# A GIN and a three-layer GAT on one core: blocks of 125 nodes, a hand-kept order, and PSUM operands for VectorE

## The chip, the cores and the metric

The kernel runs on one core of one Trainium2 chip. The metric is the device time of one execution in microseconds (us), taken as the median over several runs. A core has five engines that work side by side, each through its own list of instructions in order: PE (TensorE, matrix products; its weight loads are listed apart as PEld), DVE (VectorE), ACT (ScalarE), POOL (GpSimd) and SP (SyncE, which here only issues transfers). An instruction that waits holds up everything behind it on its engine. Transfers run on 16 DMA engines; SP and ACT issue plain ones, POOL issues those whose rows are named by a table of indices (indirect ones).

## The reference

A graph has N = 3125 nodes with 64 features and E = 103125 directed edges, sorted by destination: 50,000 random pairs in both directions and a loop at each node. Cut to what matters:

```python
h = relu(layernorm(x))
for layer in 1, 2, 3:                      # GIN, MLP widths 64, 128, 64
    agg = segment_sum(h[src] * edge_weight[:, None], dst)
    h = relu((agg + h) @ w1 + b1) @ w2 + b2      # relu between layers
x = x + h
h = relu(layernorm(x))
t = h @ init_w + init_b + mlp(pos_embed(node_vec))   # 128 features
src, dst = with_self_loops(src, dst)
for layer in 0, 1, 2:                      # GAT, 8 heads, widths 256, 256, 128
    xw = (t @ W).reshape(N, 8, C)
    logits = leaky_relu((xw * a_src).sum(-1)[src] + (xw * a_dst).sum(-1)[dst], 0.2)
    e = exp(logits - segment_max(logits, dst)[dst])
    alpha = e / segment_sum(e, dst)[dst]
    g = segment_sum(alpha[:, :, None] * xw[src], dst) + bias
    t = silu(batch_norm(g + t @ adj_w + adj_b))
return x + t @ out_w + out_b
```

## The kernel before

The node axis is cut into NT = 25 blocks of P = 128 (NP = 3200 places, the last block partly empty). The program goes through five stages.

`search` and `slots` sort the edges into slots. Nodes are ordered by their number of edges and packed into 25 groups of 128; group t has `CAPS[t]` slots per node (64 down to 23, 857 columns in all). `weigh(t)` in `slots` compares all pairs of slots of a node (128 × n × n elements on DVE) to add up the weights of repeated sources; `put(t)` then writes one column of 128 weights at a time into a dense adjacency matrix in DRAM, `adj`: 857 indirect transfers from POOL (`scatter`, L943). For GAT the slots are split again. A first edge per (node, source block) is found by a masked maximum over `key`, which gives `tops` and later `lane`: for node d and source block s the row within the block, or a mark in `void` that there is none. The edges that are left, up to 48 a node, are "the others": nodes are ordered by how many they have and packed into 25 groups of 128 with `MORE[t]` columns (44, 24, 22, ... 7; 400 in all), with row numbers in `idx` and destinations in `perm`.

`embed` (L171 to L188) makes the position embedding. `hots` turns `lane` into one-hot matrices: per destination block one DVE comparison against `iota` (L929), 25 PE transposes (L937), ACT copies (L938) and a store to DRAM by SP (L939). Both stand between `slots` and GIN in the code; within one pool the tile framework orders the instructions of each engine by a plan of its own.

`gin` keeps the sums of eight or nine destination blocks in PSUM and streams the dense adjacency past them: per layer 75 loads `adj_t` on SP's queue (L973) and matmuls with the features as weights (L977).

`gat` works in three steps per layer. First the projection: for every block `xw` and the attention terms (a row of W = D + 8 numbers), stored as a table `tab` and `ald_d` in DRAM and kept in SBUF as three bf16 parts, `split`, whose sum is the fp32 value; the dense residual goes to DRAM.

Then `add_edges`, block by block. `gather` picks the first edges' rows with one-hot matmuls: 26 slots (25 source blocks and the node's own loop) of three bf16 parts each (L1078), two slots to a PSUM tile `g`, copied to SBUF by ACT (L1079). The slots come in three parts of 12, 12 and 2 (`parts`); three large buffers `tiles` go round. `weigh` makes the weights: adds on DVE (L1088 to L1092), the leaky ReLU (L206), and in `exps` a maximum, a subtraction (L1181), the exponential on ACT (L1182) and its sum (L1180 and L1183). `add_part` multiplies the rows by the weights (L1100), adds the upper half of the slots to the lower (L1105), and lets PE add up the rest with identity matmuls into `pa` (L1107): 6 + 6 + 1 of them. The others go beside it, group by group: `others` issues POOL's fetches (L950: one `at` per group and 400 `rows` per layer, one row of W numbers per partition each) into six buffers of eight slots, `add_others` adds the terms (L1128), makes the exponentials, the products (L1100 again), the identity sums on PE (L1139), ACT's copy (L1140), and queues a scatter to `more` (L943), which POOL issues two groups later. The main loop before:

```python
for i in range(3):
    if more_:
        gather(t + 1, *nxt[i])
    add_part(pa, e, *now[i])
...
while done < NT and due[done] <= (t + 1) * due[-1] / NT:
    add_others(done, *others(done))
    done += 1
if more_:
    now, e = nxt, weigh(t + 1, nxt)
```

At last `close_rows`: the others' maxima and sums come back (`back`, L1190), both sets of sums are loaded in groups of four blocks (`got1`, `got2`, L1210), scaled (L1212), transposed and added on PE (L1221), added to the dense part (L1225, L1226), and the batch norm and SiLU follow (to L1248). A general path, for graphs that don't fit the slots, stands behind a branch and is not run.

## Time and profile before

| | us |
|---|---|
| median of 3 runs (lowest, highest) | 5104.45 (5103.35, 5113.2) |
| the profiled execution | 5023.04 |
| its span | 5021.1 |
| busy: PE, PE weight loads | 2248.5, 1675.1 |
| busy: DVE, ACT, POOL | 2020.8, 862.4, 2677.6 |

The granted TensorE clock averages 0.729. By stage, from one answer of the windows (busy us in each):

| stage | from to | length | PE | DVE | ACT | POOL |
|---|---|---|---|---|---|---|
| edges into slots, puts | 0 – 1503 | 1503 | 21 | 427 | 16 | 1057 |
| GIN (one-hots at its start) | 1503 – 1928.6 | 425.6 | 382 | 111 | 119 | 0 |
| features, projection 0 | 1928.6 – 2027 | 98.4 | 70 | 39 | 40 | 0 |
| edges of GAT layer 0 | 2027 – 3018 | 991 | 612 | 490 | 213 | 572 |
| close 0, projection 1 | 3018 – 3164 | 146 | 91 | 72 | 60 | 3 |
| edges of GAT layer 1 | 3164 – 4154 | 990 | 607 | 488 | 213 | 559 |
| close 1, projection 2 | 4154 – 4273 | 119 | 65 | 61 | 47 | 0 |
| edges of GAT layer 2 | 4273 – 4957 | 684 | 373 | 302 | 139 | 487 |
| close 2, output | 4957 – 5021 | 64 | 28 | 31 | 15 | 0 |

How to read what follows. The slices cut the span into 40 equal parts (here 125.5 us each); a digit is the busy share of an engine in tenths. A line of a timeline has the start, the length, the engine and line, the operation with out<-in, and in brackets how long the engine stood idle before it and what ended that. A line of the waits has engine, tile and line, then what released it, the idle time, how often, and the longest (us). A line of groups has the busy time, the mean in ns of one instruction, and the idle time before. Lines of the program are named L12.

### The profile page before, as it was taken

Reading aid. Unit: us, or ns where it says so; the run is one execution under the profiler, and the core shown is the slowest. Engines: PE = TensorE matmul, PEld = TensorE weight load, DVE = VectorE, ACT = ScalarE, POOL = GpSimd, SP = SyncE. Lnnn points to the kernel's source line nnn. Section 1 sums busy time; section 2 is a strip of 40 time slices with the busy share of each in tenths; the row PEclk is TensorE's granted clock in tenths of the full one; section 3 lists DMA queues with packets and bytes.
Section 4 is the critical chain, followed back from the end, with each engine's and each line's share of the span. In section 5 each row is a group of like instructions: output and inputs, shape, how many; then the busy total and the mean of one; then the engine's idle time right before and its main releaser. Section 6 shows DMA issues by size and latency. Waiting matters only on the chain. (4 is left out here: it accounts for less than half of the span.)

```text
span 5021.1 us, 36988 instructions
## 1 busy us (share of the span) xinstructions
PE 2248.5 (45%) x13235; PEld 1675.1 (33%) x13235; DVE 2020.8 (40%) x3336; ACT 862.4 (17%) x1812; POOL 2677.6 (53%) x2350
## 2 busy tenths in 40 slices
PE   0000000000008997466765665547765655456465
PEld 0000000000003333355544544436554544455464
DVE  3599202000006103355554445345653544344345
ACT  0000000000006202212211213212221213112122
POOL 2488777777770000565575540565575540677762
PEclk9555555555559997778887877778877877677787
DMA  9100000000008993433232213432232224432222
GB/s 382 61 1 0 7 1 16 0 1 1 1 1 315 363 380 142 110 85 87 84 94 78 75 52 124 103 96 87 82 93 76 76 57 122 80 79 81 73 79 69
DMA packets 235781, 465.63 MB, mean 93 GB/s; under 512 B 102719, under 2 KB 145858, under 8 KB 232386
## 3 DMA queue, kind: packets, MB, share of 16 engines
q1 hardware_dynamic: 113606, 252.99, 14.4%
q0 software_dynamic: 89424, 157.97, 13.1%
q10 hardware_dynamic: 32556, 52.20, 2.8%
q8 instruction: 106, 1.74, 0.1%
q14 instruction: 89, 0.73, 0.1%
HBM read 363.97 MB, written 99.01 MB: 92 GB/s over the span
## 5 line engine op out<-in xcount | busy, mean ns | idle before, releaser
L950 POOL DMA_INDIRECT rows<-tab,idx x1200 | 1464.7, 1221 | 831.8 <-PE pa L1139 482.9
L943 POOL DMA_INDIRECT adj<-val,celli x857 | 922.0, 1076 | 296.2 <-issue 260.3
L1078 PE MATMUL g<-split,xt 128*128 128x264 bf16 (+1 forms) x3825 | 501.4, 288 | 604.0 <-ACT xt L1079 550.8
L1078 PEld LDWEIGHTS <-xt 128*128 128x128 bf16 x3825 | 379.5, 110 | 715.2 <-issue 634.1
L977 PE MATMUL pa<-adj_t,h 128*64 128x512 f32 (+1 forms) x1050 | 280.3, 562 | 664.5 <-DMA adj_t<-adj 663.8
L950 POOL DMA_INDIRECT at<-ald,perm x75 | 73.1, 975 | 913.2 <-DVE l L1092 533.8
L1079 ACT COPY xt<-g 128x528 f32<-128x528 f32 (+1 forms) x900 | 462.5, 526 | 528.8 <-PE g L1078 293.2
L1139 PE MATMUL pa<-rows,ident 128*128 128x256 f32 (+1 forms) x2400 | 504.4, 365 | 34.5 <-ACT o L1140 24.1
L1128 DVE TENSOR_TENSOR l<-rows,at 128x64 f32<-128x64 f32 (+4 forms) x180 | 38.7, 215 | 1171.3 <-DMA rows<-tab,idx 1127.9
L1139 PEld LDWEIGHTS pa<-rows,ident 128*128 128x128 f32 x2400 | 429.5, 207 | 83.9 <-ACT o L1140 32.0
L1107 PE MATMUL pa<-xt,ident 128*128 128x256 f32 (+1 forms) x1800 | 418.6, 386 | 81.6 <-DVE xt L1105 80.9
L1100 DVE TENSOR_TENSOR xt<-xt,e 128x3072 f32<-128x3072 f32 (+1 forms) x150 | 416.4, 2817 | 0.0
L1078 PE MATMUL g<-split,hot 128*128 128x264 bf16 (+1 forms) x1800 | 246.1, 297 | 351.8 <-ACT xt L1079 295.9
L1107 PEld LDWEIGHTS pa<-xt,ident 128*128 128x128 f32 x1800 | 336.9, 217 | 135.4 <-DVE xt L1105 83.3
L977 PEld LDWEIGHTS pa<-adj_t,h 128*64 128x64 f32 x1050 | 82.9, 137 | 810.1 <-issue 744.4
L1078 PEld LDWEIGHTS <-hot 128*128 128x128 bf16 x1800 | 185.2, 113 | 405.8 <-issue 364.9
L1100 DVE TENSOR_TENSOR rows<-rows,e 128x2048 f32<-128x2048 f32 (+8 forms) x180 | 289.3, 1632 | 0.0
L175 DVE TENSOR_SCALAR em_t<-em_t,wave 128x512 f32<-128x512 f32 (+1 forms) x7 | 3.6, 515 | 659.0 <-DMA em_t<-in_node_vec 658.9
L1182 ACT ACTIVATE e<-l 128x208 f32<-128x208 f32 (+17 forms) x150 | 51.5, 343 | 1183.9 <-DVE l L1181 1183.7
L1105 DVE TENSOR_TENSOR xt<-xt 128x1536 f32<-128x1536 f32 (+1 forms) x150 | 216.5, 1485 | 0.0
L182 PE MATMUL p<-em_k,L_gnn_te_w 128*128 128x512 f32 (+1 forms) x14 | 8.7, 709 | 446.9 <-ACT em_k L180 446.9
L182 PEld LDWEIGHTS p<-em_k,L_gnn_te_w 128*128 128x128 f32 x14 | 2.8, 228 | 451.6 <-issue 450.2
(255 smaller groups left out, 2552.2 us busy)
## 6 DMA issues: line engine op xcount, KB each, us to landing
adj_t<-adj SPq DMA_DIRECT2D x150, 512.0 KB, 7.1
adj_t<-adj SPq DMA_DIRECT2D x75, 576.0 KB, 8.0
xt<-hot SPq DMA_DIRECT2D x51, 800.0 KB, 4.6
adj<-zero ACTq DMA_DIRECT2D x25, 1600.0 KB, 32.8
hot<-by_src SPq DMA_DIRECT2D x25, 800.0 KB, 4.2
hot<-hot SPq DMA_DIRECT2D x24, 800.0 KB, 4.5
rows<-tab,idx POOLq DMA_INDIRECT x1200
adj<-val,celli POOLq DMA_INDIRECT x857
```

The lines of the kernel that those rows point to most:

```text
L182: nc.tensor.matmul(p1[:, :w], w1, k, start=True, stop=True)
L943: st = self.nc.gpsimd.indirect_dma_start(out=table, out_offset=bass.IndirectOffsetOnAxis(ap=idx, axis=0), in_=row, in_offset=None)
L950: self.nc.gpsimd.indirect_dma_start(out=out, out_offset=None, in_=table, in_offset=bass.IndirectOffsetOnAxis(ap=idx, axis=0))
L977: nc.tensor.matmul(pa[i * D0 : (i + 1) * D0, c : c + w], h[:, s], tiles[i][:, c : c + w], start=s0 == 0, stop=s0 + i >= NT - 2 and i == 1,)
L1078: nc.tensor.matmul(g[:, j, :W], one, a[:, min(s, t) if s == NT else s], start=k == 0, stop=k == 2)
L1079: nc.scalar.copy(rows[:, i : i + 2], g[:, :, :W])
L1100: nc.vector.tensor_tensor(r, r, e[:, s0 : s0 + n, :, None].to_broadcast([P, n, H, C]), op=ALU.mult)
L1105: nc.vector.tensor_add(rows[:, :m, :D], rows[:, :m, :D], rows[:, m:n, :D])
L1107: nc.tensor.matmul(pa, self.ident, rows[:, j, :D], start=s0 + j == 0, stop=s0 + n == NS and j == m - 1)
L1128: nc.vector.tensor_tensor(l[:, k0 : k0 + n], rows[:, :n, D:], at[:, None, :].to_broadcast([P, n, H]), op=ALU.add)
L1139: nc.tensor.matmul(pa, self.ident, rows[:, k, :D], start=k0 + k == 0, stop=k0 + k == MORE[t] - 1)
L1182: nc.scalar.activation(e, l, AF.Exp)
```

## The change

It has five parts.

1. In `slots`, one operand of the large DVE comparisons and products is copied to PSUM by ACT (`src_p`, `wgt_p`, `order_p`, `key_p`) and read from there; the duplicate test becomes a maximum over an order instead of a sum over a mask. `hots` reads its `iota` from PSUM.
2. Embedding and one-hots get a PSUM pool of their own (`hots_ps`), and a `tc.no_sync_barrier()` stands between them and GIN: in every engine's list, what comes before it in the code stays ahead of what comes after.
3. The GAT's nodes are cut into 25 blocks of Q = 125, which is all 3125 of them, so no block is partly empty; tables, one-hots, gathers, results and closing transfers are on 125 partitions. GIN stays at 128.
4. `add_edges` is under `tc.manual_schedule()`: every engine runs in the order in which the code emits. That order is rewritten: the others of a group are weighed between the last gather part and the last sums of the block, their products and PE sums come after the block's own sums, the weights of the next block after that, and ACT's copy of the others' sums (`end_others`) last. The logits `l` and exponentials `e` are kept in PSUM where they fit (`logits`); the leaky ReLU is a product and a maximum (`bend`). The scatters to `more` lose the group that declared them independent. PSUM buffers are named afresh in one pool per step.
5. In `add_part` DVE reduces all 12 slots of the first part and six of the second to one row each, `acc` (`reduce_sum` over a transposed view, so that neighbouring elements of a sum lie W floats apart), and PE adds `acc`, the other six slots and the two last ones: 1 + 7 + 2 identity matmuls a block.

```diff
@@ slots
+            src_p = ps.tile([P, NC], F32, name="src_p")
+            nc.scalar.copy(src_p, src)
+            wgt_p = ps.tile([P, NC + CMAX], F32, name="wgt_p")
+            nc.scalar.copy(wgt_p[:, :NC], wgt)
...
+            nc.vector.tensor_scalar(order, k, -1.0, float(CMAX), op0=ALU.mult, op1=ALU.add)
+            nc.scalar.copy(wgt_p[:, NC:], order)
+            order_p = wgt_p[:, NC:]
...
-                    same, src[:, c, None].to_broadcast(wide), src[:, None, c].to_broadcast(wide), op=ALU.is_equal
-                )
-                nc.vector.tensor_tensor(part, same, earlier[:, :n, :n], op=ALU.mult)
+                    same, src[:, c, None].to_broadcast(wide), src_p[:, None, c].to_broadcast(wide), op=ALU.is_equal
+                )
+                nc.vector.tensor_tensor(part, same, order_p[:, None, :n].to_broadcast(wide), op=ALU.mult)
...
-                nc.vector.reduce_sum(again, part, axis=AX.X)
-                nc.vector.scalar_tensor_tensor(again, again, 0.0, taken[:, c], op0=ALU.is_equal, op1=ALU.mult)
+                nc.vector.reduce_max(again, part, axis=AX.X)
+                nc.vector.tensor_tensor(again, again, order_p[:, :n], op=ALU.is_equal)
+                nc.vector.tensor_tensor(again, again, taken[:, c], op=ALU.mult)
...
-                nc.vector.tensor_tensor(same, same, wgt[:, None, c].to_broadcast(wide), op=ALU.mult)
+                nc.vector.tensor_tensor(same, same, wgt_p[:, None, c].to_broadcast(wide), op=ALU.mult)
...
+            key_p = ps.tile([P, NC], F32, name="key_p")
+            nc.scalar.copy(key_p, key)
...
-                    u, key[:, None, c].to_broadcast(wide), ends[:, :, None].to_broadcast(wide), op=ALU.is_lt
-                )
-                nc.vector.tensor_tensor(u, u, key[:, None, c].to_broadcast(wide), op=ALU.mult)
+                    u, key_p[:, None, c].to_broadcast(wide), ends[:, :, None].to_broadcast(wide), op=ALU.is_lt
+                )
+                nc.vector.tensor_tensor(u, u, key_p[:, None, c].to_broadcast(wide), op=ALU.mult)
@@ hots
+        iota = ps.tile([P, P], F32, name="iota_p", bufs=1)
+        nc.scalar.copy(iota, self.iota)
...
-            wide = [P, NT, P]
+            oh = pool.tile([P, NT, P], BF16, name="oh", bufs=2)[:Q, :, :Q]
+            wide = [Q, NT, Q]
...
+                    nc.tensor.transpose(pt[:Q, i, :Q], oh[:, s0 + i], self.identb[:Q, :Q])
+                nc.scalar.copy(by_src[:, s0 : s0 + n, :Q], pt[:Q, :n, :Q])
+            nc.sync.dma_start(self.hot[t], by_src.rearrange("p s d -> p (s d)"))
@@ scatter
+            if group:
+                self.tc.declare_no_dep(st.ins, group=group, reason="each has a row of its own")
@@ gat
-                    nc.sync.dma_start(tab[t0 * P : (t0 + S) * P].rearrange("(t p) d -> p t d", p=P), row)
-                    self.store_rows(ald_d, ald, t0, t0 + S)
+                    for table, rows in ((tab, row), (ald_d, ald[:, t0 : t0 + S])):
+                        nc.sync.dma_start(table[t0 * Q : (t0 + S) * Q].rearrange("(t p) d -> p t d", p=Q), rows)
...
+            with tc.tile_pool(name=f"gat_sum{layer}", bufs=2) as io, tc.tile_pool(
+                name=f"gat_ps_sum{layer}", bufs=1, space=PSUM
+            ) as ps, tc.manual_schedule():
                 self.add_edges(io, ps, layer, D, xt, yt, split, ald, stat, tab, ald_d, res, more)
@@ add_edges
+            nc.sync.dma_start(hot[t % 3][:Q], self.hot[t])
...
+                g = ps.tile([P, 2, BLK], F32, name="g", tag="g", bufs=2)
...
+                        nc.tensor.matmul(g[:Q, j, :W], one, a[:, t if s == NT else s], start=k == 0, stop=k == 2)
+                nc.scalar.copy(rows[:, i : i + 2], g[:Q, :, :W])
...
+        def logits(name, n, rows=P):
+            a = ps.tile([P, BLK], F32, name=name, tag=name)[:rows]
+            half = BLK // 2
+            e = a[:, BLK - n * H :] if n * H > half else a[:, half : half + n * H]
+            l = io.tile([P, n * H], F32, name=f"l{name}", bufs=1)[:rows] if n * H > half else a[:, : n * H]
+            return (v.rearrange("p (k h) -> p k h", h=H) for v in (l, e))
+
+        def bend(l, n):
+            z = io.tile([P, RMAX, H], F32, name="z")[: l.shape[0], :n]
+            nc.vector.tensor_scalar(z, l, SLOPE, None, op0=ALU.mult)
+            nc.vector.tensor_tensor(l, l, z, op=ALU.max)
...
         def add_part(pa, e, s0, n, rows):
             times(rows, e, s0, n)
-            m = n // 2
-            nc.vector.tensor_add(rows[:, :m, :D], rows[:, :m, :D], rows[:, m:n, :D])
-            for j in range(m):
-                nc.tensor.matmul(pa, self.ident, rows[:, j, :D], start=s0 + j == 0, stop=s0 + n == NS and j == m - 1)
+            m = (n, n // 2, 0)[s0 // HALF]
+            add = [rows[:, j, :D] for j in range(m, n)]
+            if m:
+                acc = io.tile([P, D], F32, name="acc")[:Q]
+                nc.vector.reduce_sum(acc, rows[:, :m, :D].rearrange("p k d -> p d k"), axis=AX.X)
+                add.append(acc)
+            for j, a in enumerate(add):
+                nc.tensor.matmul(
+                    pa, self.ident[:Q, :Q], a, start=s0 + j == 0, stop=s0 + n == NS and j == len(add) - 1
+                )
...
-            late.append((more, [(o, self.perm[:, t : t + 1])], f"more{layer}"))
+            late.append((more, [(o, self.perm[:, t : t + 1])], None))
...
             for i in range(3):
-                if more_:
+                if ahead:
                     gather(t + 1, *nxt[i])
+                if i == 2:
+                    weighed = None
+                    while done < NT and due[done] <= t * due[-1] / NT:
+                        if weighed:
+                            end_others(*add_others(*weighed))
+                        weighed = weigh_others(done, *others(done))
+                        done += 1
                 add_part(pa, e, *now[i])
...
-            while done < NT and due[done] <= (t + 1) * due[-1] / NT:
-                add_others(done, *others(done))
-                done += 1
-            if more_:
+            added = weighed and add_others(*weighed)
+            if ahead:
                 now, e = nxt, weigh(t + 1, nxt)
+            if added:
+                end_others(*added)
@@ close_rows
-        res, more = (a.rearrange("(t p) d -> p t d", p=P) for a in (res, more))
+        res, more = (a[:N].rearrange("(t p) d -> p t d", p=Q) for a in (res, more))
...
+        for b, t0 in enumerate(range(0, NT, 4)):
+            n = min(4, NT - t0)
+            c0, w = t0 * Q, n * Q
@@ fast
-        with tc.tile_pool(name="fgin_ps", bufs=2, space=PSUM) as k.ps:
+        with tc.tile_pool(name="hots_ps", bufs=3, space=PSUM) as k.ps:
...
                 k.hots(hp, k.ps)
+
+        tc.no_sync_barrier()
+        with tc.tile_pool(name="fgin_ps", bufs=2, space=PSUM) as k.ps:
```

## The prediction

> **What bounds the kernel now.** I read the slices first, to find stages that one engine fills, then the windows of each stage, then the waits inside the longest, then the queue that holds up the next.
>
> ```profile
> DVE  3599202000006103355554445345653544344345
> POOL 2488777777770000565575540565575540677762
> DMA  9100000000008993433232213432232224432222
> ```
>
> Three stages. Up to 1503 us POOL runs without a break: 857 puts into the adjacency and 50 other scatters, 0.97 us each with 0.30 us of issue between. Then GIN, with the DMA engines full. From 2000 us the three GAT layers, with no engine full.
>
> In the first stage a put is longer whenever a DVE instruction with two SBUF operands runs beside it. POOL's and DVE's timelines around 854 us:
>
> ```profile
> 851.65 0.97 POOL L943 DMA_INDIRECT adj<-val,celli  x1 [0.30 <-issue]
> 854.31 4.57 POOL L943 DMA_INDIRECT adj<-val,celli  x1 [0.30 <-issue]
> ...
> 850.75 1.82 DVE L122 TENSOR_REDUCE ln_v<-ln_sq 128x25 f32<-128x1600 f32 x1
> 854.55 3.49 DVE L929 TENSOR_TENSOR oh<-lane,iota 128x3200 bf16<-128x3200 f32 x1
> ```
>
> The put beside the one-source reduce keeps its 0.97 us; the one beside L929 waits it out. Summed over POOL's timeline from 243 us on, the excess over 0.97 us is 99 us, 88 of it before 560 us, while DVE builds the slots.
>
> GIN's start is the SP queue's:
>
> ```profile
> 1503.21 7.11 SPq L973 DMA_DIRECT2D adj_t<-adj  x8
> 1510.42 0.38 SPq L171 DMA_DIRECT2D em_t<-in_node_vec  x1
> ...
> 1554.36 5.04 SPq L939 DMA_DIRECT2D hot<-by_src  x2
> ...
> 1657.41 249.93 SPq L973 DMA_DIRECT2D adj_t<-adj  x174
> 1928.61 0.33 SPq L1015 DMA_DIRECT2D gw<-in_L_gnn_gat_w  x1
> ```
>
> The adjacency loads stand in the queue from 846 us until the last put lands, and the embedding's loads behind them; so 23 of 25 blocks of one-hots are made and stored while GIN wants the DMA engines.
>
> Inside GAT layer 0, and for layer 2 (half as wide), the windows and the waits:
>
> ```profile
> 2027.00:3018.00 991.00, 611.52 (x3316) 488.02 (x3314) 489.99 (x571) 213.34 (x413) 571.67 (x450) 0.80 0.30 81
> 4273.00:4957.00 684.00, 373.22 (x3313) 357.41 (x3312) 301.81 (x570) 139.06 (x413) 486.88 (x450) 0.75 0.30 74
> ...
> ACT e L1182 <- DVE l L1181: 440.1, 46, 47.6
> DVE l L1128 <- DMA rows<-tab,idx: 390.3, 56, 12.8
> PE g L1078 <- ACT xt L1079: 345.5, 31, 47.6
> POOL rows L950 <- PE pa L1139: 222.8, 22, 18.8
> ```
>
> Per block 39.6 us, of which PE works 24.5, DVE 19.6, POOL 22.9. It is a chain of orders: DVE stands at L1128 until POOL's rows land; ACT stands at the exponential that DVE owes, with the copies of the next gather behind it; PE stands for those copies; POOL for row buffers that PE has not read.
>
> **The change, part by part.** Sums are against the profiled execution (span 5021.1, time 5023.04 us). The median of the runs shown, 5104.45, is 81.4 us above it; I carry that difference unchanged.
>
> *PSUM operands in the slots.* One input of every large comparison and product (src, wgt, order, key) moves to PSUM. [...] by the row the 99 us less what still has two inputs (small products, layer norm, embedding; I leave 19). I take −80. The price: four ACT copies of 857 columns and about 0.05 us per DVE instruction (0.73 at L185 with PSUM against 0.68 at L178); POOL waits for DVE only once there (35.3 us), so at most 3 us.
>
> *The fence.* Embedding and one-hots run between 840 and 1500 us, where PE, ACT and DVE are idle; their SP stores go ahead of the adjacency loads. 174 loads were issued in 249.9 us once the one-hots were out, 1.436 us each; 225 take 323, plus 7 to the first landing and 21 from the last issue to L1015: 351 against 425, −74. The cover is POOL's puts; the one-hots are hidden only if their DVE instruction, with iota in PSUM, leaves puts alone: else 23 × 3.6 = 83 us come back.
>
> *GAT, 256 wide: DVE.* L1105 goes: 85.5 + 10.5 = −96. In its place two reduces per block over slots 1056 bytes apart. The nearest row is a strided one:
>
> ```profile
> 135.59 3.14 DVE L746 TENSOR_REDUCE pl<-run 128x25 f32<-128x1625 f32 x1
> ...
> L1105 DVE TENSOR_TENSOR xt<-xt 128x1536 f32<-128x1536 f32 x50 | 85.5, 1752 | 0.0
> ```
>
> 1.84 ns per element and 0.15 fixed, against 1.08 in a contiguous one (L829, 4.43 us for 4096). So 5.8 + 3.0 us × 25 = +220 (contiguous +130). The leaky ReLU in two instructions, each as long as L1181, instead of L206 adds 0.7 us per block, 17; some 21 small instructions per block with PSUM operands, 0.06 each, 32. 490 − 96 + 220 + 17 + 32 = 663, with DVE's waits for its exponentials (20) 683: 27.3 us per block.
>
> *PE.* Ten sums per block instead of thirteen, 0.46 us each: 611 − 34 = 577. [...] the bounds are nothing and the f32 load's 218 ns against 107 (L1107, L1078), which would lift a gather matmul from 152 to at most 195 ns: +84, 661, still under DVE.
>
> *POOL.* With the exponentials in PSUM the large products leave POOL alone: 450 × 1.25 = 563, no longer 572 plus 108 of issue.
>
> *The order.* On PE the first gather part, the one sum of `acc`, the second part and so on; on DVE the others' weights ahead of the last part; on ACT every copy of the block's gather ahead of the exponentials. Walked through from DVE's start of a block: first reduce done at 9.2, PE's first part done at 5.3, so `acc` waits; second part at 15; second reduce at 15.5; others' rows weighed at 18; products at 23; next weights at 27.3; PE's last sums at 28.6, where its next first part takes until 34, still ahead of DVE's 36.5. DVE never waits for PE, and for POOL only where rows are late: 22.5 against 27.3 us, and six row buffers hold two blocks. So DVE sets the period: 683, plus 10 of start, 35 of tail (two small blocks of others, their scatters, which now each wait for the one before): 728 against 991, −263 in each of two layers.
>
> *GAT, 128 wide.* DVE 302 − 53 + 114 + 17 + 32 + 20 = 432, PE at most 540 (373 − 20, and 187 if all its weight loads were slow): POOL is left as the bound. 563, plus 10 while block 0's 44 rows hold all six buffers, plus 35 of tail: 608 against 684, −76.
>
> *Blocks of 125.* Hot loads and stores, result, table and got transfers change from 128 to 125 partitions. In the trace 128 partitions give 16 four-byte completions. [...] the last store, 53 partitions, moves its 256-byte packets one after another, 14 ns apart. [...] Hot loads, 25 packets of 0.25 us: 6 us, prefetched a block ahead, hidden. In the closing loop 1024-byte packets take 46 ns: 1250 per engine are 57.5, with dense 7.8 and back 6.9: 72 us against 48 now, +24 (128 wide: 45 against 31, +14). Table stores +3 per layer. Sum +71; with 16 engines still, 0. I take +71.
>
> Sum: −80 − 74 − 526 − 76 + 71 = −685. Span 4336; median 5104.45 − 685 = 4419.
>
> **The rivals.**
> *Reduces at full rate.* L746's rate is stride; should 1056 bytes cost nothing, DVE falls to 593 and PE, 577 to 661 with its waits, sets about 660 per layer: −65 twice, 4290. Against it: L1180, another strided reduce, gains 0.44 us from 104 elements to 352, 1.78 ns each.
>
> *The PSUM operand does not free POOL* (the change not doing what it says). Then −80 is lost, the one-hots cost 83, layer 2 is bound by 450 × 1.38 = 622, +55; the wide layers at 450 × 1.60 = 720 stay near 760, +60. 4700. Only the reduce speaks against it; no large DVE instruction with a PSUM input ran beside POOL before.
>
> *Order losses.* Late rows or PSUM buffers held single cost 5 us per block in 50 blocks, 250: 4670.
>
> *Engines in turn* (slower). PE's `acc` stands ahead of its second part, and that waits for DVE's reduce; if DVE in turn waited for each part, a block would be 24 + 27 = 51 us: 1333 per wide layer, 31 × 25 + 45 = 820 in layer 2. −80 − 74 + 684 + 136 + 71: 5840. The other parts bring 83 net, so it decides from 83/50 = 1.7 us above today's 39.6 us per block; the walk above is 12 below.
>
> **The numbers.** Forecast 0.55, full-rate reduces 0.12, no relief 0.12, order losses 0.13, in turn 0.07; 0.01 for no change, within 0.2% (about 10 us, what runs of this kernel can tell apart). Faster 0.92, slower 0.07. The range from 4240 (full-rate reduces[...]) to 4700 leaves out "in turn" and the edges of the others.
>
> **What would show it.** Puts of 0.97 us throughout, GIN starting near 1425 and lasting 350; one-hots before 1100. In the wide layers DVE over 90% busy, first reduce at 5.8 us, L1128's wait for rows nearly gone, 29 us per block. In layer 2 POOL at 1.25 per fetch without gaps. Five completions per 125-partition transfer, and a closing loop of 72 us. Wrong if DVE still stands for rows or copies, if POOL's fetches stay at 1.3 us in GAT, or if the reduces take 3.4.

## The result: 5804 us against 5105, and the profile after

| | before | changed |
|---|---|---|
| median of 4 runs each (lowest, highest), us | 5104.99 (5103.35, 5113.2) | 5804.68 (5794.31, 5813.85) |
| profiled execution, span | 5021.1 | 5804.3 |

The ratio is 1.137, 95% interval 1.134 to 1.139: slower, where a gain was forecast (4419, range 4240 to 4700). The number comes near that of the rival "engines in turn" (5840), but not for its reason.

The slices of the changed kernel (40 of 145 us each):

```profile
DVE  4647620000210126555555436456456444343353
POOL 2574777777400032333433102443343304434451
DMA  9000000000179652222222223222222223111112
```

POOL, busy for 572 of 991 us in the edges of GAT layer 0 before, is busy for 427 of 1149 here, DVE is no nearer to 90%, and GIN's block of full DMA starts later. The windows of GAT layers 0 and 2:

```profile
2111.00:3260.00 1149.00, 648.75 (x3241) 557.63 (x3239) 622.78 (x597) 223.88 (x425) 427.33 (x450) 0.76 0.26 69
4794.00:5717.00 923.00, 399.27 (x3171) 374.30 (x3168) 379.23 (x594) 143.50 (x414) 426.33 (x450) 0.66 0.22 55
```

No engine has more work than the prediction gave it: DVE 623 us (forecast 663), PE 649 (577 to 661), POOL's fetches 0.945 us each. Yet the layer takes 1149. The waits in layer 0:

```profile
PEld L1103 <- issue: 389.6, 120, 33.6
DVE o L1241 <- ACT le L1240: 340.4, 23, 47.5
POOL rows L967 <- PE pa L1186: 332.3, 10, 102.2
ACT xt L1104 <- remote: 274.4, 38, 16.2
PE g L1103 <- issue: 235.8, 51, 34.0
```

"issue" and "remote" are waits that no instruction of the trace explains. Instructions of the trace wait on semaphores, and it has records of raises of these: by an instruction (in the kernel before 9 to 14 ns after its end, by the medians of ACT, DVE and PE) and by a transfer that lands (16 for a put). I call each raise an update. ACT's timeline of the gather's copies, then PE's of the matmuls that feed them, then POOL's, show when these waits occur:

```profile
2542.88 0.60 ACT L1104 COPY xt<-g 125x528 f32<-125x528 f32 x1 [0.85 <-PE g L1103]
2546.43 0.60 ACT L1104 COPY xt<-g 125x528 f32<-125x528 f32 x1 [2.95 <-remote]
2552.06 0.60 ACT L1104 COPY xt<-g 125x528 f32<-125x528 f32 x1 [5.03 <-issue]
2562.58 1.10 ACT L1104 COPY xt<-g 125x528 f32<-125x528 f32 x2 [9.93 <-remote]
2564.75 0.60 ACT L1104 COPY xt<-g 125x528 f32<-125x528 f32 x1 [1.07 <-PE g L1103]
2566.07 0.60 ACT L1104 COPY xt<-g 125x528 f32<-125x528 f32 x1 [0.72 <-PE g L1103]
```

```profile
2543.53 0.83 PE L1103 MATMUL g<-split,xt 125*125 125x264 bf16 x6 [0.61 <-issue]
2547.08 0.84 PE L1103 MATMUL g<-split,xt 125*125 125x264 bf16 x6 [2.71 <-issue]
2552.71 1.48 PE L1103 MATMUL g<-split,xt 125*125 125x264 bf16 x6 [4.36 <-issue]
```

```profile
2534.38 0.94 POOL L967 DMA_INDIRECT rows<-tab,idx  x1 [21.65 <-PE pa L1186]
...
2558.18 0.97 POOL L967 DMA_INDIRECT at<-ald,perm  x1 [0.30 <-issue]
2583.91 0.94 POOL L967 DMA_INDIRECT rows<-tab,idx  x1 [24.76 <-PE pa L1186]
```

From 2534 to 2559 POOL issues fetches back to back. ACT's copies stand for 3, 5 and 10 us, and start some 2, 4 and 8 us after the matmuls they need are done (2544.4, 2547.9 and 2554.2). Soon after POOL stops, ACT's waits are 0.7 to 1.1 us. Then POOL stands 25 us for row buffers, which PE frees late. So POOL and the PE–ACT pair do take turns, here 25 us each.

The hand-kept order is not needed for this, for the one-hots, outside that region, do the same beside the puts:

```profile
913.59 0.99 ACT L953 COPY by_src<-pt 125x1000 bf16<-125x1000 bf16 x1 [20.63 <-remote]
935.99 0.99 ACT L953 COPY by_src<-pt 125x1000 bf16<-125x1000 bf16 x1 [21.41 <-issue]
958.38 0.99 ACT L953 COPY by_src<-pt 125x1000 bf16<-125x1000 bf16 x1 [21.41 <-remote]
961.19 0.27 ACT L953 COPY by_src<-pt 125x125 bf16<-125x125 bf16 x1 [1.81 <-PE pt L952]
```

A copy of eight transposes comes 22.4 us after the one before it, a copy of one transpose 2.8 us after: 2.8 us for each of PE's updates. DVE's chains of small instructions in the slots go on at multiples of 0.7 us, mostly 1.4 or 2.8 (starts at 344.2, 347.7, 350.5 and 353.3, for instance). I call these late updates. The trace marks them in another way too. These are its records of POOL's DMA landings (each put ends in 16), counted from the start of the span:

```
landings recorded per 20 us   260-280  300-320  340-360  500-520      560-580  640-660
kernel before                    192      176      230      112          240      233
changed kernel                   256      166       24     0 (no puts)   240       16
```

In the changed kernel nine tenths of them are missing from 340 us on, they are back after a pause of POOL (468 to 532, in which it waits for DVE's late chain), and gone again 80 us later. The puts kept their usual 1.27 us, though in the trace each waits for a semaphore of the eighth put before it; so those landings came in time, and it is their records that are missing, and the other engines' updates that are late. The granted clock is no rival: it is 0.76 in layer 0, and 0.90 where the same program ran undisturbed (below), but that adds 56 us to PE's busy time and nothing to the other engines', while the layer grows by 391.

The one-hots were done at 1650 us instead of the forecast 1100, and the fence made GIN wait for them: its loads start at 1653, not 1503.

### The profile page after: what moved, and what is told of

It reads as the page before. It is cut to its first block, busy times and chain, and to the rows that moved or that the text cites. A ratio compares the mean times of both kernels' runs of the same rounds, so it can differ in the third digit from the quotient of the medians.

```text
span 5804.3 us, 36599 instructions
## 1 busy us (share of the span) xinstructions
PE 2399.0 (41%) x12785; PEld 1893.2 (33%) x12785; DVE 2370.4 (41%) x3438; ACT 876.1 (15%) x1819; POOL 2297.4 (40%) x2350
## 5 line engine op out<-in xcount | busy, mean ns | idle before, releaser
L967 POOL DMA_INDIRECT rows<-tab,idx x1200 | 1133.8, 945 | 1251.3 <-PE pa L1186 882.0
L1103 PE MATMUL g<-split,xt 125*125 125x264 bf16 (+1 forms) x3825 | 551.4, 305 | 769.1 <-issue 463.8
L1103 PEld LDWEIGHTS <-xt 125*125 125x125 bf16 x3825 | 505.6, 170 | 819.3 <-issue 797.5
L1104 ACT COPY xt<-g 125x528 f32<-125x528 f32 (+1 forms) x900 | 468.0, 528 | 1497.8 <-remote 924.1
L1147 DVE TENSOR_REDUCE acc<-xt 125x256 f32<-125x3072 f32 (+3 forms) x150 | 537.3, 3582 | 14.8
L1103 PE MATMUL g<-split,hot 125*125 125x264 bf16 (+1 forms) x1800 | 262.0, 304 | 421.0 <-issue 238.1
L1138 DVE TENSOR_TENSOR xt<-xt,le 125x3072 f32<-125x3072 f32 (+1 forms) x150 | 421.7, 2811 | 0.0
L1103 PEld LDWEIGHTS <-hot 125*125 125x125 bf16 x1800 | 236.6, 169 | 447.9 <-issue 440.8
L943 DVE TENSOR_TENSOR oh<-lane,iota_p 125x3125 bf16<-125x3125 f32 x25 | 85.3, 3411 | 670.4 <-PE pt L952 638.7
L1138 DVE TENSOR_TENSOR rows<-rows,le 128x2048 f32<-128x2048 f32 (+8 forms) x180 | 284.3, 1627 | 0.0
L1150 PE MATMUL pa<-xt,ident 125*125 125x256 f32 (+1 forms) x900 | 215.7, 401 | 4.8 <-DVE xt L1138 4.8
```

The source lines that it names most:

```text
L943: nc.vector.tensor_tensor(oh, self.lane[:Q, t, :, None].to_broadcast(wide), iota[:Q, None, :Q].to_broadcast(wide), op=ALU.is_equal,)
L967: self.nc.gpsimd.indirect_dma_start(out=out, out_offset=None, in_=table, in_offset=bass.IndirectOffsetOnAxis(ap=idx, axis=0))
L1103: nc.tensor.matmul(g[:Q, j, :W], one, a[:, t if s == NT else s], start=k == 0, stop=k == 2)
L1104: nc.scalar.copy(rows[:, i : i + 2], g[:Q, :, :W])
L1138: nc.vector.tensor_tensor(r, r, e[:, s0 : s0 + n, :, None].to_broadcast([*r.shape[:3], C]), op=ALU.mult)
L1147: nc.vector.reduce_sum(acc, rows[:, :m, :D].rearrange("p k d -> p d k"), axis=AX.X)
```

## The experiments

**Without PSUM operands.** The edit (one place of several; key, order and iota in the same way):

```diff
-            src_p = ps.tile([P, NC], F32, name="src_p")
-            nc.scalar.copy(src_p, src)
+            src_p = src
...
+            l, e = (io.tile([P, RMAX * H], F32, name=f"{m}{name}", bufs=1)[:rows, : n * H] for m in "le")
```

> The changed kernel with every PSUM operand of DVE back in SBUF: src, wgt, order, key, iota and the GAT's logits and exponentials. Order, blocks of 125, reduces and fence stay. Three theories of why the changed kernel takes 5804 us. Late updates: while POOL issues indirect DMAs back to back (0.95 to 0.97 us with 0.30 between), the other engines see each other's semaphore updates late, 1.4 us for each of DVE's and 2.8 us for each of PE's, whatever the operands; two-source DVE instructions in SBUF slow POOL down, and the updates come in time again. PSUM reads: the delay comes from DVE's own PSUM accesses beside POOL. Order: the hand-kept order makes DVE wait for exponentials behind ACT's copies, with no delay of updates at all. By late updates and by PSUM reads: one-hots done well before the last put, GIN from about 1510 us, POOL's fetches at 1.2 to 1.4 us, wide GAT layers 700 to 900 us, 4500 to 4900 in all. By order alone: wide layers stay over 1100 us, 5600 or more.

4740.24 us against 4987.16 for the kernel before on that chip: 0.950 (0.948 to 0.951). The wide layers take 806 us, a fetch 1.27 us on average, and no landing is missing. I took this to rule out the order; it could not, as will be seen, because on this chip nothing came late in any run.

**A chain of small DVE instructions beside the puts**, in the kernel before, once in SBUF and once in PSUM (and two PSUM buffers fewer for `pp`, for room):

```diff
             for t in range(8, NT):
                 put(t)
+            fill = sp.tile([P, NT, 20], F32, name="fill")    # or ps.tile
...
+            for _ in range(200):
+                nc.vector.reduce_sum(sums, fill, axis=AX.X)
+                nc.vector.tensor_copy(fill[:, :, 0], sums)
```

> The kernel before, with 400 extra small DVE instructions in a dependent chain (a reduce of 128x25x20 and a copy of its 25 sums back into its source, by turns), all in SBUF, placed when the slots are done, beside POOL's puts at 0.97 us with 0.30 between; their result is not used. Without delay a pair takes about 0.8 us, 160 us for all, and DVE has nothing else to do there. Late updates: the chain falls to about 1.4 us per update, 500 us or more, and the DMA landings in the trace thin out, after some tens of us. PSUM reads: 160 us, nothing thins out. The time stays near that of the kernel before in both cases, since the puts cover it.

> As the run with the chain in SBUF, but the chain's source lies in PSUM (each pair reads 500 elements from PSUM and writes 25 back). Late updates: the same as with SBUF, some 500 us. PSUM reads: 500 us here alone. Neither, if both chains take about 160 to 180 us: then it takes PE or ACT, or both engines at once, to make the updates late.

Both chains took 196 us and no landing was missing. By these two runs neither theory held: nothing was late.

**A slower POOL in GAT**, in the changed kernel:

```diff
+    def pace(self):
+        self.nc.gpsimd.memset(self.spacer, 0.0)      # spacer: 128x320
...
                     self.fetch(rows[:, k], tab, self.idx[:, t, k0 + k : k0 + k + 1])
+                    self.pace()
```

> The changed kernel with a POOL memset of 128x320 (about 0.35 us) behind every row fetch of the GAT layers, so that a fetch comes every 1.9 us instead of 1.25. Late updates: the indirect DMAs are no longer back to back; PE's and ACT's gather goes on beside them, ACT's waits of 3 to 16 us in the gather vanish, and although POOL has 0.65 x 16 = 10 us more per block, a wide layer takes 800 to 900 us instead of 1150, the whole 5000 to 5200. PSUM reads or order: the waits stay, POOL's part of each block is 10 us longer, wide layers 1300 to 1400 us, the whole 6300.

4572.66 us. The gain was larger than forecast, and more came to light than the edit can do: the first stages, whose code it leaves alone, had no late updates either, with all landings recorded and the one-hots done at 992 us. The kernel before took 4987 there, not 5105.

**The changed kernel again, on other chips.**

> The changed kernel as it is, on the chip of these runs. In the paced run the first stage, which has the same code as the changed kernel up to the GAT layers, showed none of the late updates (256 landings per 20 us all through, one-hots done by 1040 us). Two theories are left. The program makes the updates late: something in the program as compiled (its order of instructions in all) sets them off from 310 us on, and this run takes 5750 to 5850 us again. The run made them late: the executions of the first result were disturbed as a whole, the same program shows prompt updates here, and takes what its own instructions add up to, 4400 to 4600 us, less than the paced one's 4573 by up to 150.

> The paced kernel again, timed, on the same chip as the changed kernel. If the program makes the updates late, 4573 as before and the changed kernel 1200 us above. If the run made them late, the memset behind every fetch costs something or nothing here: POOL has 16 x 1.9 = 31 us per block with it, DVE 27 by the prediction's sum, so 4573 against 4450 or so without.

> The changed kernel as it is, once more. The chip of the first four runs (where the kernel before takes 4987 us) showed no late updates in the first stage of the paced kernel; the chip of the last two (kernel before: 5104) showed them in the same stage of the same program. If the kernel before takes about 4987 beside this run, the theory that the chip's state decides says 4400 to 4550 us for the changed kernel; the theory that the program alone decides says 5800 on any chip. If the kernel before takes about 5104, both say 5800.

> The kernel before, for its trace on the chip of this set. Where it takes 5104 us: the landings in the trace thin out in the GAT layers and at the end of the puts, and each of the three layers is 20 to 40 us longer than in the trace of before (991, 990, 684), which is the 80 us between its median and its profiled execution. Where it takes 4987: all landings are there, and the layers take 985 and 680.

> The changed kernel as it is, in search of a chip on which the updates come in time. Where the kernel before takes about 4987: 4400 to 4550 us, all landings in the trace. Where it takes about 5104: 5800 again.

These runs fell on five chips; which chip the first result came from is not recorded. The three kernels on each (us; medians where timed, else one run):

| chip | before | changed | paced | late updates |
|---|---|---|---|---|
| 12 | 4987 | – | 4573 | none |
| 14 | 4996 | 4466 | – | none |
| 13 | 5104 | 5801 | 4819 | yes |
| 5 | 5100 | 5798 | – | yes |
| 7 | 5123 | – | – | yes |

The last column is read from the traces: on chips 12 and 14 at least 99.8% of the landings of POOL's transfers are recorded in every run, in the changed kernel on chips 13 and 5, as in the first result, 22%. (Chip 7 shows it in the runs below.) On chip 14 the same program takes 4466 us, 0.894 of the kernel before (one run): near the forecast. On chips 13 and 5 it takes 5800, as in the first result. So the first four runs, all on chip 12, say nothing of the cause. On chip 13 the memset alone takes 982 us off the changed kernel, both timed, and brings its wide layers from 1148 and 1139 us to 770 and 767: there POOL's pace is a cause. ACT's timeline of the one-hots on chip 14, beside puts at the same pace:

```profile
882.64 2.95 ACT L953 COPY by_src<-pt 125x1000 bf16<-125x1000 bf16 x4 [3.69 <-DMA hot<-by_src]
889.32 2.95 ACT L953 COPY by_src<-pt 125x1000 bf16<-125x1000 bf16 x4 [3.73 <-DMA hot<-by_src]
```

Four copies in 2.95 us, a block every 6.7 us instead of 70. And the windows of the three GAT layers there:

```profile
1884.00:2642.00 758.00, 592.73 (x3237) 508.68 (x3235) 624.28 (x597) 225.06 (x425) 427.20 (x450) 0.90 0.41 105
2848.00:3605.00 757.00, 589.67 (x3241) 505.19 (x3239) 624.26 (x598) 225.25 (x425) 427.36 (x450) 0.90 0.41 105
3784.00:4378.00 594.00, 352.23 (x3176) 333.13 (x3173) 380.21 (x594) 144.74 (x415) 426.92 (x450) 0.78 0.39 85
```

DVE and POOL are busy for the same time as in the first result, and layer 0 is 391 us shorter. DVE is at 82%.

The kernel before on chip 5 (5115.93 us in this run) suffers as well, where DVE's small instructions meet the first puts, and in the narrow layer: the last put ends at 1524 us, that layer takes 746 us against 680 on chip 14. The wide layers, 993 and 998 us, hardly change (991 and 990), against the expectation, though half of their landings' records are missing.

```profile
399.46 0.20 DVE L880 MAX8 row<-key 128x8 f32<-128x39 f32 x1 [2.54 <-remote]
402.26 0.20 DVE L880 MAX8 row<-key 128x8 f32<-128x38 f32 x1 [2.60 <-issue]
```

```profile
4305.00:5051.00 746.00, 384.18 (x3301) 356.06 (x3301) 302.63 (x565) 140.98 (x411) 483.66 (x450) 0.71 0.26 68
```

(The first fence is DVE's timeline, the second the window of the narrow layer.) The trace of before has all its landings; against it, these two places (27 and 62 us) make 89 of the 93 us by which this run is longer. The median of before, 82 us above its profiled execution, is thus most likely that of a chip with late updates; no trace of those runs is on record.

**The chain and the operands on chips with late updates.**

> The kernel before with the chain of 400 small DVE instructions in SBUF beside the puts, again. On the first chip a pair took 0.98 us and no landing was missing. Load theory: on the slower chips semaphore updates have a ceiling of about 13 per us; POOL's puts alone make 12.6 (16 per 1.27 us), and whatever comes on top tips them over. There the chain's 2.5 updates per us tip it: within 50 us landings fall to some 50 per 40 us and each link takes 1.4 us or more, the chain 600 us instead of 196, with no PSUM and no PE in it. If it takes PE or PSUM: 196 us on any chip.

> The kernel before with the chain of 400 small DVE instructions in SBUF beside the puts. On both chips where the kernel before takes 4987 to 4996 us it took 195 us and no landing was missing. Where the kernel before takes about 5104, load theory: the chain takes 600 us or more and landings fall to some 50 per 40 us while it runs, although it uses neither PSUM nor PE. If it takes PE or PSUM: 195 us.

> The changed kernel with all PSUM operands back in SBUF (4740 us on the chip of the first runs). Late updates by back-to-back indirect DMAs: where the kernel before takes 5104, DVE's two-source instructions slow POOL in the GAT layers and while one-hots are made, so the updates stay mostly prompt: wide layers 800 to 850, GIN from 1540, 4750 to 4900 in all, about 1000 less than the changed kernel. If late updates had nothing to do with POOL's pace: 5600 or more. Where the kernel before takes 4987: 4740 again.

On chip 14 the chain took 196 us again, on chip 7 478 us. The lines of its reduces, on chip 14 and then on chip 7, have their lengths in ns (least, median, most) and the starts of the first and the last; the last two lines say how long DVE stood for which instruction of the chain (us, times):

```profile
L905 DVE TENSOR_REDUCE fill_sums<-fill x200: 668/676/676, 814.8 to 1009.5; 128x25 f32<-128x500 f32 x100
```

```profile
L905 DVE TENSOR_REDUCE fill_sums<-fill x200: 667/675/676, 865.9 to 1342.1; 128x25 f32<-128x500 f32 x100
...
  DVE fill L906: 150.9, 130
  DVE fill_sums L905: 96.9, 129
```

The instructions are as long as before (0.675 us); most wait for the one ahead. From 700 to 860 us the puts alone, at full pace, had their landings recorded (1994 of 2000). The chain starts at 866; from 880 to 920 us 120 of 512 were left, then 33 of 496. From 1400 to 1550 us no engine but POOL works any more, and still only 217 of 1776 are recorded. So one engine's updates on top of back-to-back indirect DMAs are enough to start it, without PSUM and without PE, and once begun it stays while the puts alone go on. That is the load theory's sign; the size was smaller than its 600 us, and its ceiling of about 13 updates per us was my estimate from the puts' 12.6, which no run measured. PSUM reads are not needed for it.

Without PSUM operands the changed kernel took 5072.61 us on chip 5: 725 less than the changed kernel there, 332 more than on chip 12, and above the 4750 to 4900 expected. DVE's two-source instructions slow POOL (a fetch takes 1.24 us on average, not 0.945), and the wide layers take 834 and 838 us, but the one-hots crawled all the same, to 1678.

**A shorter pause.** As the paced kernel, with a memset of 128x64:

> The paced kernel with a memset of 128x64 (about 0.15 us) instead of 128x320. A fetch every 1.4 us makes 11.4 landings per us, in place of 9.8 with the longer memset and 12.8 without. Where the kernel before takes 5104: if the load alone decides, the wide layers fall between 770 (long memset) and 1148 (none), 900 or so, 5100 to 5300 in all; if any gap on POOL is enough, 770 again and 4800. Where it takes 4990: DVE sets the wide layers as without a memset, 757, and the narrow one 620; 4495.

5825.95 us on chip 7, wide layers 1152 and 1150: no better than none. POOL's timelines show why. First the short memset, then the long one of the paced kernel on chip 13:

```profile
2537.84 0.17 POOL L968 MEMSET spacer<- 128x64 f32 x1
2538.17 0.95 POOL L971 DMA_INDIRECT rows<-tab,idx  x1 [0.16 <-issue]
2539.12 0.17 POOL L968 MEMSET spacer<- 128x64 f32 x1
2539.45 0.95 POOL L971 DMA_INDIRECT rows<-tab,idx  x1 [0.16 <-issue]
```

```profile
2535.80 0.38 POOL L968 MEMSET spacer<- 128x320 f32 x1
2536.35 0.96 POOL L971 DMA_INDIRECT rows<-tab,idx  x1 [0.17 <-issue]
2537.30 0.38 POOL L968 MEMSET spacer<- 128x320 f32 x1
2537.85 0.95 POOL L971 DMA_INDIRECT rows<-tab,idx  x1 [0.17 <-issue]
```

Half of the gap between two fetches disappears beside the memset: a fetch every 1.28 us with the short one (1.25 without any), every 1.50 us with the long one, not 1.40 and 1.90 as I had reckoned. So a memset as such does nothing; the pace must fall. For this gather the edge lies between 12.5 landings per us (16 / 1.28) and 10.7: wide layers 1152 us on the one side, on the other 770 and 767 on chip 13, and 797 and 789 on chip 7 (in a run with cut transfers, below), against 763 without late updates. On the paced side about half of the landings' records are still missing, so the edge is not sharp.

**Without the fence:** `tc.no_sync_barrier()` taken out.

> The changed kernel without the fence between one-hots and GIN. Where the kernel before takes 5104: one-hots are no longer waited for while the puts make them slow; GIN's loads start at 1535 instead of 1653 but share the DMA engines with the one-hots' stores again, so GIN ends some 40 to 80 us earlier than with the fence: 5730 to 5770. Where it takes 4987, the one-hots are hidden with the fence, and without it 70 to 80 us are lost.

5876.47 us on chip 5, 79 more than with it, against the expectation: GIN's loads start at 1538, but stand between the one-hots' stores, which last until 1745, and are all issued only at 2055 instead of 1975.

**Transfers cut in two**, on top of the paced kernel (table stores, `back` and both `got` loads; here one):

```diff
-                nc.sync.dma_start(a[:, :n], part[:, t0 : t0 + n, :D])
+                for c in (slice(0, 112), slice(112, Q)):
+                    nc.sync.dma_start(a[c, :n], part[c, t0 : t0 + n, :D])
```

> The paced kernel with each transfer of the result, table and statistics over 125 partitions cut in two, of 112 and 13 partitions. If 125 partitions use five engines[...], the time between the end of a layer's edges and the next layer's first fetch (205 and 179 us in the paced run, 141 and 119 in the kernel before) comes back to 145 to 155 and 120 to 130, the end from 86 to 65 to 70: 120 to 140 us less than the paced kernel in all (4819 where the kernel before takes 5104, 4573 where it takes 4987). If the engines' number does not matter: nothing, or slower by the additional issues (some 0.3 us each, 90 of them).

> The paced kernel with the cut transfers, timed. On the chip with 4996 for the kernel before it took 4444 in one run. Where the kernel before takes 5104: 4819 less 140, so 4680, a version that beats both kernels on either kind of chip. Where it takes 4990: 4445 again, 110 above the version with the cut alone.

> The changed kernel with the cut transfers and without the memsets. Where the kernel before takes about 4990: 4466 less 130, so 4335 (the memsets cost 7 us in each wide layer and 96 in the narrow one there). Where it takes 5104: the updates are late and 5670 is what is left of 5800.

4444.18 us on chip 14, only 22 less than the changed kernel there. The four stretches between the stages (last GIN load to the first fetch, from layer to layer twice, and the end) fall from 138, 206, 180 and 86 us in the changed kernel there to 121, 157, 135 and 66: 131 us. The memsets take most of it back, above all in the narrow layer (691 us against 594). The first scaling of layer 0, with what it waited for, in the changed kernel (the load is issued at 2642) and in the cut one (issued at 2630):

```profile
2667.88 0.37 DVE L1251 TENSOR_TENSOR m<-stat,back 125x200 f32<-125x200 f32 x1 [32.38 <-DMA back<-gat_more]
```

```profile
2639.91 0.37 DVE L1259 TENSOR_TENSOR m<-stat,back 125x200 f32<-125x200 f32 x1 [18.19 <-DMA back<-gat_more]
```

26 us against 10 for the same bytes. Timed on chip 7, the paced and cut kernel takes 4756.66, 0.929 of the kernel before (0.927 to 0.931), where 4680 was expected; with the cut alone 5695.73, 1.112 (1.110 to 1.115). So pace and cut together beat the kernel before on either kind of chip. Against the changed kernel the gain is shown only where updates are late: on chip 14 there is one run each, 4444 and 4466, and seven runs of the kernel before spread by 36 us there. The cut without the pace was not run on a chip without late updates.

**The first stages as before**, with pace and cut:

> The paced kernel with the cut transfers, and with the first stages as in the kernel before: no PSUM operands in the slots and one-hots, no pool of their own, no fence. Where the kernel before takes 5104, the one-hots no longer crawl beside the puts in front of GIN: the adjacency loads end at 1935 as in the kernel before instead of 1975, so 40 us less than the cut version, 4620 to 4680. Where it takes 4987, the fence's and the operands' gain is given away: 140 us more than the cut version, about 4590.

4662.34 us on chip 14, 0.935 (0.932 to 0.937), 218 more than the cut kernel; some 4590 were expected. The two-source operands cost 60 us of it (last put 1475 against 1416) and the order without a fence the rest: GIN's last load at 1970 against 1744, later than the kernel before (1889), so this is not quite its first stage.

## Why the prediction was wrong

The step that failed is the walk through a block of the wide layers: "DVE never waits for PE, and for POOL only where rows are late", and from it "So DVE sets the period: 683, plus 10 of start, 35 of tail", 728 us. It put the time between the end of an instruction and the moment when another engine learns of it at nothing. In the first result, while POOL issued at full pace, it was 2.8 us for each of PE's updates at the one-hots and 2 to 8 us before ACT's copies in the gather; over layer 0 DVE stood 340 us for exponentials and POOL 332 for row buffers, and the layer took 1149.

A sign of it stood at the head of the sum: "The median of the runs shown, 5104.45, is 81.4 us above it; I carry that difference unchanged." 1.6% between two measurements of a kernel whose runs there agree within 0.2% was no constant. By the times on the five chips it was a cost of late updates, and the change multiplied it: it brings a fetch of the wide layers from 1.29 us on average to 0.945 and lets PE, ACT and DVE work beside it.

Here the prediction stage by stage, against the two kernels side by side on chip 14 (the one before with the chain, hidden beside the puts) and on chip 5:

| step | forecast | chip 14 | chip 5 |
|---|---|---|---|
| last put (PSUM operands) | −80 | −61 | +6 |
| GIN from first to last load, and what precedes it (fence) | −74 | −83 | +36 |
| two wide layers | −526 | −461 | +299 |
| narrow layer | −76 | −86 | +173 |
| 125 partitions, between the stages | +71 | +168 | +168 |
| sum | −685 | −524 | +682 |

The sums are the differences of the traces' spans, 523.9 and 681.8 us; the terms are rounded.

*PSUM operands.* Right as to what they do: on chip 14 puts take 0.97 us in the median beside L829, L874 and the one-hots' L943, each with one of its operands in PSUM; in the kernel before, the put beside the one-hots' comparison with both in SBUF took 4.57. What I had not asked is what an unhindered POOL sets off: that DVE slowed the fetches (1.29 us on average in layer 0, 0.945 in the changed kernel) had been a pace-maker. On chip 5 the gain was lost again while POOL stood 64 us for DVE's late chain (38 on chip 14).

*Fence.* Right on chip 14: GIN from 1424 to 1746, 322 us. On the other chips the cover that I named ("the cover is POOL's puts") was itself what made the one-hots slow.

*Wide layers.* 758 against 728 on chip 14. The reduces take 5.7 and 2.9 us (forecast 5.8 and 3.0), in the middle of the layer a block takes 27.9 us on DVE (27.3). DVE's own work came out 39 us below the 663, but at the start it waits 47 us for the first block's copies (10 in the sum), and 56 us for exponentials of the others (20). The rival of full-rate reduces falls. The bf16 weight load of 125 columns does take longer, 0.137 us in the median (0.098 with 128, both in layer 0 on chip 14), but inside the bounds that I had estimated from the trace (nothing more, or as much as the f32 load), and off the path.

*Narrow layer.* 594 against 608.

*125 partitions.* The forecast's 25 and 1250 packets per engine rest on five engines, which the trace of before does not show for 125 partitions; the traces of the changed kernel do. On chip 14, as in the first result, the load of `back` ends in five 4-byte packets, with 128 partitions in sixteen; in the first result the 1024-byte packets of layer 0's `got` loads run most often five at a time (39 of 67 us), in the kernel before sixteen or seventeen (9 of 25 us). The cut to 112 and 13 gives most of the loss back (131 us between the stages). The size came out more than double: closing was counted by its packets at 72 us; it took 93. The 64-byte packets of `back`, put at 6.9 us, took 26 in front of everything else, for the first 2000 packets of `got` went out at the same time: 35 us of the one and 97 of the other, which over five engines is some 26 (an estimate from the trace's packets). The table stores, put at 3 us a layer, take 18 or so with what waits behind them.

*"Engines in turn".* Its price was right by chance (and its 1333 us needs 51.5 us a block, not the rounded 51, which make 1320). PE's sums of `acc` wait only 68 us in layer 0 on chip 14. What takes turns is POOL on one side and PE with ACT on the other, and with prompt updates they don't.

What stays open: why the chips differ (12 and 14 had none of it, 13, 5 and 7 all of it), and whether tracing has a part in it. Every execution here was recorded by the profiler, so no run can tell.

## What to carry to other kernels

When the profiled execution and the timed runs of a kernel differ by more than the runs among themselves, find out where before predicting: the same program on another chip may have another bottleneck. A queue that is freed from contention runs into whatever it had been held back from, so ask what its full pace loads (here fetches of 0.945 us instead of 1.29, and a layer of 1149 us instead of 991). Where engines hand over small pieces beside a stream of indirect DMAs, a pause in the stream (here 0.25 us per fetch) can be worth more than the stream's speed: 982 us on a chip with late updates, at a price of some 107 on a chip without (4573 against 4466, one run each on two chips).

## What the runs showed of the hardware

- On three of five chips, semaphore updates arrived late while POOL issued indirect DMAs every 1.25 to 1.28 us and another engine updated semaphores: 2.8 us for each of PE's, mostly 1.4 or 2.8 in DVE's chains. At one every 1.50 us the wide layers took 767 to 797 us instead of 1149. Once begun, it stayed while the puts alone went on (217 of 1776 landings recorded), and after a pause of POOL (468 to 532 us in the first result) the landings were recorded again, 240 in 20 us; on the other two chips it did not occur.
- A POOL memset of 0.17 us between two indirect DMAs cost 0.03 us, one of 0.38 cost 0.25: about 0.14 us of the 0.30 between them disappear.
- A load of 125 partitions with 64-byte packets took 26 us beside other loads, in two pieces of 112 and 13 partitions 10; with 128 partitions, in the kernel before, 6.5.
